# Two-layer graph attention: denominators summed into a row per target, own rows scaled on ScalarE, edge products ahead of weight copies

## The chip, the cores and the metric

The kernel runs on one core of a Trainium2 chip. The metric is the device time of one execution in microseconds; the median of several runs is compared.

## The reference

Two graph-attention layers run over 3327 nodes with 1024 features. Each layer adds its input to its output and normalizes every row.

```python
# layer 0, 8 heads of 128 features; adj has about 0.5% ones and ones on the diagonal
h = (x @ W0).reshape(C, 8, 128)
e = leaky_relu(alpha_src[:, :, None] + alpha_dst[:, None, :], 0.2)   # per head, C x C
attn = softmax(where(adj == 0, -inf, e), axis=-1)
x = layernorm(x + attn @ h)
# layer 1, one head
h = x @ W1
e = leaky_relu(h @ a1 + (h @ a2).T, 0.2)
x = layernorm(x + relu(softmax(where(adj > 0, e, -9e15), axis=1) @ h))
```

Since leaky_relu is a maximum of two linear terms, exp of it is a maximum of two products, so that the kernel needs an exponential only once per node and head, and multiplies and takes a maximum per edge.

## The kernel before

Nodes are cut into 26 tiles of 128 rows (`NT`). A tile of rows whose outputs are computed is called a target. The adjacency matrix is sparse, so the kernel first makes lists of edges, and then works edge by edge. There are three stages.

**Projection** (to about 552 us). For every tile, x is turned on TensorE and multiplied by W0 (L546), the result goes to `h0_d` in DRAM, and VectorE builds the edge lists `idx` and `tgt`. When half of the tiles are projected, a generator (`sums_so_far`) is run a step at a time between matmuls: for each of the first 13 targets (`EARLY`) it gathers the first two of the five edge blocks, sums the weighted rows into PSUM (L671), copies them to `z` (L726) and writes them to `half_d`; the softmax denominators of these blocks go to `dens`.

**Layer 0** (552 to about 1171 us). The order of the targets alternates between a late one (tiles 13 to 25, five blocks of edges) and an early one (tiles 0 to 12, three blocks left). A block is four gathers of 128 rows of `h0_d` (indirect DMAs issued by GpSimd, L1033); the last block, `EB`, is one gather. Five block buffers go round; a buffer is refilled when TensorE has finished with it. The instruction order of each engine is the order in which the code issues (`manual_schedule`), and every engine works its queue in order. For each target:

- `prepare` loads x rows and the target's own rows of `h0_d`, for an early one also the part sum `half_d`; `marks` (L1049, L1053) compares target numbers and gives the one-hot `oh`.
- `own` gives the weight `es` of each row for itself. For a late target ScalarE scales the own rows in eight steps (L1092); for an early one VectorE scales them and adds the part sum in eight steps (L1088). TensorE adds the result to the accumulators with an identity matmul, a half at the second and a half at the third block (L1126).
- `weights` makes a block's edge weights in the PSUM tile `way` (L1109, L1110), ScalarE copies them to `w` (L1112), and VectorE multiplies them with the one-hot to `e` (L1114).
- `sums` multiplies `e` with the gathered rows (L1145; L1134 for the last block) and sums the denominators (L1155, L1138): `w` is the stationary side, `oh` moves, so the result `den` has a row for each of 4 groups x 8 heads and a column for each target.
- `finish` masks the entries of `den` that do not belong together (L1167, `meets`), sums them by a matmul with `heads` (L1168) into a row per target, takes the reciprocal (L1171, L1172), scales the accumulators and adds x (L1177), normalizes, makes the two scores for layer 1 (L1184) and stores to `y_d`. It is a generator: `plans` says after which block of the next targets its next step is issued.

The same mask and heads matmul stand in `sums_so_far` (L707, L740, L737; L719 for the sums of denominators), put off to the next target by `owed`.

**Layer 1** (1171 to the end) gathers rows of `y_d` in the same way, sums them, and multiplies by W1 (L1289).

The two places that the change touches most, in the code before:

```python
den = ph.dd[:, P : 2 * P + H]                       # in sums_so_far
nc.tensor.matmul(den[: NG * H, :P], made[b][0].rearrange("p g h -> p (g h)"),
                 oh[:, b * NG : (b + 1) * NG, :].rearrange("p g t -> p (g t)"), ...)
```

Of the kernel before, what the change touches and what calls it, by code (L numbers as in the profile page):

```python
# [9 lines left out]
F32 = mybir.dt.float32  # L10
# [16 lines left out]
def kernel(  # L27
# [103 lines left out]
    io_t = const.tile([P, P], F32, name="io_t")  # L131
    meets = const.tile([NG * H, P], F32, name="meets")
    heads = const.tile([NG * H, H], F32, name="heads")

# [379 lines left out]
    with ExitStack() as own, tc.manual_schedule():  # L514
# [114 lines left out]
        def sums_so_far():  # L629
# [62 lines left out]
            yield  # L692
            owed = None
            for s in range(EARLY):
                acc = part.bank("L", [P, 2, 4, DH], "part")
                made = []
                for b in range(HB):
                    n = s * HB + b
                    val = src[n % 3]
                    made.append(weights(val, b, res[0], oh))  # L700
                    yield
                    if n:
                        fetch(n + 2)
                    yield
                    if b == 0 and owed:
                        met = part.sbuf("met", [NG * H, P], 1)
                        nc.vector.tensor_tensor(met, den[: NG * H, :P], meets, OP.mult)  # L707
                    yield
                    sums(acc, val, b, made[b][1], range(H // 2))
                    yield  # L710
                    sums(acc, val, b, made[b][1], range(H // 2, H))
                    if b == 0:
                        yield
                        if owed:
                            owed()
                        yield
                den = ph.dd[:, P : 2 * P + H]
# [21 lines left out]
            met = part.sbuf("met", [NG * H, P], 1)  # L739
            nc.vector.tensor_tensor(met, den[: NG * H, :P], meets, OP.mult)  # L740
            owed()

# [127 lines left out]
        for t in range(3, NT):  # L870
# [13 lines left out]
            if t == 11:  # L884
                ph.iota([P, P], [[1, P]], "io_t", base=1, dst=io_t)
                same = ident[: NG * H, : NG * H].rearrange("p (g h) -> p g h", g=NG)
                met = meets.rearrange("p (g t) -> p g t", g=NG)
                nc.vector.tensor_reduce(met[:, :, 0], same, AX.X, OP.max)
                nc.vector.tensor_copy(met[:, :, 1:], met[:, :, :1].to_broadcast([NG * H, NG, GT - 1]))
                nc.vector.tensor_reduce(heads, same.rearrange("p g h -> p h g"), AX.X, OP.max)  # L890
            if t == 16:
# [79 lines left out]
    def sparse(own):  # L971
# [84 lines left out]
        class Layer0:  # L1056
# [20 lines left out]
            def own(self):  # L1077

                t, h = self.t, self.h
                es = self.es = sbuf("es0", [P, H], 2)  # L1080
                nc.scalar.activation(es, sd0[:, t, 0, :], AF.Exp, scale=1 - SLOPE)
                nc.vector.tensor_tensor(es, es, h[:, D : D + H], OP.mult)
                nc.vector.tensor_tensor(es, es, h[:, D + H :], OP.max)
                nc.vector.tensor_scalar(es, es, loop[:, t : t + 1], None, op0=OP.mult)
                for n in range(H):
                    d = slice(n * DH, (n + 1) * DH)
                    if t < EARLY:
                        nc.vector.scalar_tensor_tensor(  # L1088
                            h[:, d], h[:, d], es[:, n : n + 1], self.half[:, d], op0=OP.mult, op1=OP.add
                        )  # L1090
# [11 lines left out]
            def weights(self, b):  # L1102
# [7 lines left out]
                nc.vector.tensor_tensor(wp, wp, s[:, :, D + H : D + 2 * H], OP.max)  # L1110
                w = sbuf("w", [P, NG, H], 4)
                nc.scalar.activation(w, wp if b < EB else wp.to_broadcast([P, NG, H]), AF.Copy)  # L1112
                e = sbuf("e", [P, H * P], 3).rearrange("p (g h t) -> p g h t", g=ng, h=H)
                nc.vector.tensor_tensor(  # L1114
                    e, oh.unsqueeze(2).to_broadcast([P, ng, H, wide]),
                    wp.unsqueeze(3).to_broadcast([P, ng, H, wide]), OP.mult,
                )
                self.made[b] = w, e

            def sums(self, b):  # L1120
# [4 lines left out]
                if j in (1, 2):  # L1125
                    nc.tensor.matmul(  # L1126
                        self.acc[j - 1].rearrange("p h d -> p (h d)"), ident, self.h[:, (j - 1) * HALF : j * HALF],
                        start=False, stop=False,
                    )
                elif j == 3:  # L1130
                    nc.tensor.matmul(self.acc[0][:, 0, :1], ident_b, none_b, start=False, stop=False)
                if b == EB:
                    for h in range(H):
                        nc.tensor.matmul(  # L1134
                            self.acc[h // 4][:, h % 4, :], e[:, 0, h, :], rowsof[:, 0, h, :],
                            start=False, stop=h % 4 == 3,
                        )
                    nc.tensor.matmul(  # L1138
                        self.den[: NG * H, :P], w.rearrange("p g h -> p (g h)"), self.oh2, start=False, stop=True
                    )  # L1140
                    return
# [10 lines left out]
                if j == 1:  # L1152
                    self.den = bank("S", [P, P + H], "den")
                for n in self.blocks[:2] if j == 1 else (b,):
                    nc.tensor.matmul(  # L1155
                        self.den[: NG * H, :P], self.made[n][0].rearrange("p g h -> p (g h)"),
                        self.oh[:, n * NG : (n + 1) * NG, :].rearrange("p g t -> p (g t)"),
                        start=n == self.blocks[0], stop=False,
                    )

# [3 lines left out]
            def finish(self):  # L1164

                met = sbuf("met", [NG * H, P], 2)
                nc.vector.tensor_tensor(met, self.den[: NG * H, :P], meets, OP.mult)  # L1167
                nc.tensor.matmul(self.den[:, P:], met, heads, start=True, stop=True)  # L1168
# [32 lines left out]
        class Target:  # L1201
# [21 lines left out]
            def own(self):  # L1223
# [5 lines left out]
                )  # L1229
                nc.vector.tensor_tensor(es[:, :1], es[:, 1:], loop[:, t : t + 1], OP.mult)  # L1230

            def fetch(self, b):
# [88 lines left out]
        def pipeline(items, fetches):  # L1321

            left, sent = [], [0]
            plans = {
                len(Target.blocks): ((), (2, 1), (1,), (1,), (1,), (1,)),
                len(Target.blocks) - HB: ((), (2, 1, 1), (1, 1), (1,)),
                Target: ((2,), (2, 1), (2, 1), (1, 1), (1, 1), (1,)),
# [30 lines left out]
            for i, it in enumerate(items):  # L1358
# [4 lines left out]
                for j, b in enumerate(it.blocks):  # L1363
                    if j == 0 and i:
                        items[i - 1].close()
                        if turn:
                            for _ in range(5):
# [189 lines left out]
```

## Time and profile before

| | us |
|---|---|
| median of 11 runs | 1801.81 (1797.72 to 1807.09) |
| the profiled execution's own time | 1803.52 |
| its span, first to last instruction | 1801.8 |

| stage (us) | length | PE busy | DVE busy | ACT busy | POOL busy | PE clock | GB/s |
|---|---|---|---|---|---|---|---|
| 280 to 552, projection with part sums | 272 | 259.4 | 220.4 | 126.4 | 184.6 | 0.99 | 281 |
| 570 to 690, layer 0 | 120 | 81.5 | 100.7 | 25.5 | 79.8 | 0.80 | 411 |
| 690 to 1090, layer 0 | 400 | 285.4 | 312.5 | 102.2 | 259.5 | 0.75 | 395 |
| 1090 to 1171, end of layer 0 | 81 | 41.7 | 40.9 | 14.7 | 49.7 | 0.77 | 338 |
| 1171 to 1801, layer 1 | 630 | 623.1 | 275.6 | 74.4 | 407.9 | 1.00 | 367 |

PE is TensorE's matmuls, PEld its weight loads, DVE VectorE, ACT ScalarE, POOL GpSimd, SP the engine that issues plain DMAs. "PE clock" is the share of full speed that the chip granted to TensorE. Lines such as L1114 are those of the kernel before. In the groups of instructions, `out<-in` names the tiles by the program's names. In the waits, "A <- B" says that A's engine sat idle until B had ended; the numbers are the total in us, how many times, and the longest. In the chain and the timeline, the first number is the start and the second the length. A float32 matmul appears as two passes, so "x2" is one matmul of the program.

### The profile page before, as it was taken

The page shows a single profiled execution, that of the slowest core. Times are in us where ns is not written, and L with a number is a line of the kernel's source. Part 1 is how long each engine was busy: PE and PEld are TensorE (multiplying, and loading weights), DVE is VectorE, ACT ScalarE, POOL GpSimd, SP SyncE. Part 2 cuts the span into 40 slices and gives each one's busy share as a digit, 9 for nine tenths or more (in the row PEclk, how much of TensorE's full clock was granted, in tenths as well). Part 3 has the DMA queues.
Part 4 walks back from the last instruction along what each step waited for, and adds up shares of the span by engine and source line. Part 5 has one row for each costly group of instructions (what it writes and reads, how often), then busy time and mean ns, then how long its engine had stood idle before and what let it go on. Part 6 is the DMA issues. An engine that isn't in the chain of part 4 may idle for free.

```text
span 1801.8 us, 35565 instructions
## 1 busy us (share of the span) xinstructions
PE 1548.4 (86%) x13168; PEld 909.3 (50%) x13168; DVE 1186.8 (66%) x3262; ACT 512.3 (28%) x1519; POOL 1109.8 (62%) x1580
## 2 busy tenths in 40 slices
PE   8899989999994677667777666499999999999998
PEld 4566656666663555455555454144444444444443
DVE  5799998898865888777777777344444444444443
ACT  5666654554431222222222222111111111111110
POOL 4533346677745766666666665677777667676650
PEclk9999999999996887867787768699999999999999
DMA  7456859999779999999999999999999999999980
GB/s 191 90 118 125 161 113 297 256 297 293 272 260 359 412 411 403 388 393 401 398 394 400 395 393 329 352 403 403 399 397 386 401 405 398 379 393 393 388 347 35
DMA packets 187319, 586.89 MB, mean 326 GB/s; under 512 B 36641, under 2 KB 46651, under 8 KB 187136
## 3 DMA queue, kind: packets, MB, share of 16 engines
q0 software_dynamic: 131056, 457.74, 71.3%
q1 hardware_dynamic: 55922, 126.52, 18.9%
q8 instruction: 107, 1.75, 0.4%
q14 instruction: 76, 0.62, 0.1%
q10 hardware_dynamic: 158, 0.26, 0.0%
HBM read 587.80 MB, written 51.23 MB: 355 GB/s over the span
## 4 chain that ended last, share of the span: by engine, by line
PE 55%; DMA 17%; DVE 15%; issue 5%; ACT 4%; POOL 3%; DVEq 0%; SPq 0%; ACTq 0%; POOLq 0%
PE mm L1289 21%; PE acc L1257 13%; PE mm L546 11%; DMA src<-h_d,idx 7%; DMA near<-h_d,idx 4%; PE acc L1145 3%; PE part L671 2%; PE tr L197 2%; ACT junk L350 2%; DVE e L1114 2%; PE acc L1126 1%; DMA own<-h_d 1%; DMA wt<-in_L_gnn_W_dram 1%; DVE top L309 1%; DMA src<-y_d,idx 1%
## 5 line engine op out<-in xcount | busy, mean ns | idle before, releaser
L546 PE MATMUL mm<-wt,xT 128*128 128x347 f32 (+1 forms) x1248 | 412.8, 472 | 3.4 <-DMA wt<-in_L_gnn_W_dram 3.4
L1289 PE MATMUL mm<-wt,xT 128*128 128x512 f32 x832 | 387.6, 604 | 0.0
L1033 POOL DMA_INDIRECT src<-y_d,idx x256 | 260.3, 1017 | 124.7 <-PE acc L1257 40.8
L546 PEld LDWEIGHTS mm<-wt,xT 128*128 128x128 f32 x1248 | 227.0, 193 | 120.6 <-issue 23.7
L1033 POOL DMA_INDIRECT src<-h_d,idx x184 | 196.7, 1069 | 110.2 <-PE acc L1145 23.2
L1289 PEld LDWEIGHTS mm<-wt,xT 128*128 128x128 f32 x832 | 149.7, 189 | 198.6 <-issue 193.6
L1292 DVE SCALAR_TENSOR_TENSOR o<-mm,y 128x512 f32<-128x512 f32 x52 | 36.0, 692 | 315.2 <-PE mm L1289 315.2
L1033 POOL DMA_INDIRECT near<-y_d,idx x160 | 163.7, 1023 | 61.5 <-issue 22.1
L1033 POOL DMA_INDIRECT near<-h_d,idx x120 | 131.1, 1093 | 70.0 <-PE acc L1145 21.1
L1114 DVE TENSOR_TENSOR e<-oh,way 128x1024 f32<-128x1024 f32 x104 | 127.1, 1222 | 58.7 <-ACT w L1112 58.3
L1145 PE MATMUL acc<-src,e 128*32 128x128 f32 x2944 | 124.4, 339 | 37.9 <-issue 19.2
L1257 PE MATMUL acc<-src,es 128*32 128x342 f32 (+1 forms) x1536 | 128.8, 470 | 25.4 <-DVE es L1248 25.4
L1145 PEld LDWEIGHTS acc<-src,e 128*32 128x32 f32 x2944 | 106.2, 138 | 72.4 <-issue 31.5
L200 ACT ACTIVATE xT<-tr 128x512 f32<-128x512 f32 x104 | 62.3, 600 | 249.3 <-PE tr L197 249.3
L1271 ACT ACTIVATE z<-y,ri 128x342 f32<-128x342 f32 (+1 forms) x78 | 39.5, 569 | 297.9 <-DVE ri L1267 297.9
L1145 PE MATMUL acc<-near,e 128*32 128x128 f32 x2048 | 88.8, 346 | 41.0 <-issue 18.1
L1112 ACT ACTIVATE w<-way 128x32 f32<-128x32 f32 x104 | 20.2, 194 | 330.0 <-DVE way L1110 324.9
L1145 PEld LDWEIGHTS acc<-near,e 128*32 128x32 f32 x2048 | 76.2, 141 | 66.2 <-issue 44.4
L641 POOL DMA_INDIRECT near<-h_d,idx x76 | 82.8, 1090 | 27.4 <-issue 18.3
L1257 PEld LDWEIGHTS acc<-src,es 128*32 128x32 f32 x1536 | 44.4, 112 | 98.4 <-issue 45.5
L1168 PE MATMUL den<-heads,met 32*128 32x8 f32 x52 | 14.2, 343 | 87.6 <-DVE met L1167 87.6
L350 ACT ACTIVATE junk<-ad 128x1664 uint8<-128x1664 uint8 x52 | 82.5, 1586 | 4.7 <-POOL ad L339 3.4
(247 smaller groups left out, 2587.9 us busy)
## 6 DMA issues: line engine op xcount, KB each, us to landing
h_d<-ht SPq DMA_DIRECT2D x26, 520.0 KB
own<-h_d SPq DMA_DIRECT2D x26, 520.0 KB
y_d<-y SPq DMA_DIRECT2D x26, 514.0 KB
y<-y_d SPq DMA_DIRECT2D x26, 514.0 KB
x<-in_x_dram SPq DMA_DIRECT2D x25, 512.0 KB
y<-in_x_dram SPq DMA_DIRECT2D x25, 512.0 KB
out_dram<-o SPq DMA_DIRECT2D x25, 512.0 KB
ad<-in_adj_dram POOLq DMA_DIRECT2D x25, 415.9 KB
```

Source lines behind the costliest of these rows:

```text
L197: nc.tensor.transpose(tr[:, k, :], src[:, (4 * g + k) * P : (4 * g + k + 1) * P], ident)
L200: nc.scalar.activation(part, tr, AF.Copy)
L350: nc.scalar.activation(junk, ad[:, n * THR : (n + 1) * THR], AF.Copy, accum_out=self.d[:, n : n + 1])
L546: nc.tensor.matmul(acc, xT[t][:, k, :], wt[:, k, CUTS0[c] : CUTS0[c + 1]], start=k == 0, stop=k == KT - 1)
L641: nc.gpsimd.indirect_dma_start(out=src[n % 3][:, g, :], out_offset=None, in_=h0_d[:THR, :], in_offset=bass.IndirectOffsetOnAxis(ap=idx[:, ...
L671: nc.tensor.matmul(acc[g * GT : (g + 1) * GT, h // 4, h % 4, :], e[:, g, h, :], vals[:, g, h, :], start=b == 0 and h % 4 == 0, stop=b == H ...
L1033: nc.gpsimd.indirect_dma_start(out=s[:, g, :w], out_offset=None, in_=table[:n, :], in_offset=bass.IndirectOffsetOnAxis(ap=idx[:, t, b * NG ...
L1114: nc.vector.tensor_tensor(e, oh.unsqueeze(2).to_broadcast([P, ng, H, wide]), wp.unsqueeze(3).to_broadcast([P, ng, H, wide]), OP.mult,)
L1145: nc.tensor.matmul(self.acc[h // 4][g * GT : (g + 1) * GT, h % 4, :], e[:, g, h, :], rowsof[:, g, h, :], start=first and h % 4 == 0, stop= ...
L1257: nc.tensor.matmul(self.acc[c][to, :m], es[:, g, :], s[:, g, CUTS[c] : CUTS[c + 1]], start=b == 0, stop=b == EB,)
L1271: nc.scalar.activation(z[:, cut], self.res[:, cut], AF.Copy, scale=ri[:, 1:2])
L1289: nc.tensor.matmul(acc, xT[:, k, :], wt1[:, k, half], start=k == 0, stop=k == KT - 1)
```

## The change

Four things are changed together.

- **Denominators.** One-hot marks are now the stationary side and the weights move, group by group: four matmuls of 8 columns for each block write a row per target. The constants `meets` and `heads`, the masks and the heads matmuls go, in layer 0 and in the projection's part sums; there `dens` is copied by ScalarE directly after `z`. `finish` has one step fewer, and `plans` and the count of steps at the turn to layer 1 are fitted to it.
- **Own rows.** They are scaled in eight steps by ScalarE for all targets, in a method `scale_own` that is issued after the weights of the second block. For an early target the part sum `half` is no longer added on VectorE: two more identity matmuls add it into the accumulators. The sum `es + dens` goes to a tile of its own, `total`.
- **Exponentials.** Those of `es` are made once for all targets at the start of layer 0 (`grows`).
- **Products.** `e` is issued before the copy `w`. Both read the PSUM tile `way`, and the program keeps the two engines apart there: the copy now waits for the product, and the next block's first write into `way` waits for the copy.

```diff
                 den = ph.dd[:, P : P + H]                      # sums_so_far
                 for b in range(HB):
-                    nc.tensor.matmul(
-                        den[: NG * H, :P], made[b][0].rearrange("p g h -> p (g h)"),
-                        oh[:, b * NG : (b + 1) * NG, :].rearrange("p g t -> p (g t)"),
-                        start=b == 0, stop=b == HB - 1,
-                    )
+                    for g in range(NG):
+                        nc.tensor.matmul(
+                            den[g * GT : (g + 1) * GT, :], oh[:, b * NG + g, :], made[b][0][:, g, :],
+                            start=b == 0, stop=b == HB - 1,
+                        )
...
                     nc.scalar.activation(z[:, n], acc[:, n], AF.Copy)
+                nc.scalar.activation(dens[:, s, :], den, AF.Copy)
...
-                def owed(s=s):
-                    nc.tensor.matmul(den[:, P:], met, heads, start=True, stop=True)
-                    nc.scalar.activation(dens[:, s, :], den[:, P:], AF.Copy)
...
+        grows = pool.tile([P, NT, H], F32, bufs=1, name="grows")
+        nc.scalar.activation(grows, sd0[:, :, 0, :], AF.Exp, scale=1 - SLOPE)
...
             def own(self):
-                es = self.es = sbuf("es0", [P, H], 2)
-                nc.scalar.activation(es, sd0[:, t, 0, :], AF.Exp, scale=1 - SLOPE)
-                nc.vector.tensor_tensor(es, es, h[:, D : D + H], OP.mult)
+                es, total = sbuf("es0", [P, 2, H], 2).rearrange("p a h -> a p h")
+                nc.vector.tensor_tensor(es, grows[:, t, :], h[:, D : D + H], OP.mult)
                 nc.vector.tensor_tensor(es, es, h[:, D + H :], OP.max)
                 nc.vector.tensor_scalar(es, es, loop[:, t : t + 1], None, op0=OP.mult)
+                self.es = self.total = es
+                if t < EARLY:
+                    self.total = total
+                    nc.vector.tensor_tensor(total, es, dens[:, t, :], OP.add)
+
+            def scale_own(self):
+                h = self.h
                 for n in range(H):
                     d = slice(n * DH, (n + 1) * DH)
-                    if t < EARLY:
-                        nc.vector.scalar_tensor_tensor(
-                            h[:, d], h[:, d], es[:, n : n + 1], self.half[:, d], op0=OP.mult, op1=OP.add
-                        )
-                    else:
-                        nc.scalar.activation(h[:, d], h[:, d], AF.Copy, scale=es[:, n : n + 1])
-                if t < EARLY:
-                    nc.vector.tensor_tensor(es, es, dens[:, t, :], OP.add)
+                    nc.scalar.activation(h[:, d], h[:, d], AF.Copy, scale=self.es[:, n : n + 1])
...
             def weights(self, b):
-                w = sbuf("w", [P, NG, H], 4)
-                nc.scalar.activation(w, wp if b < EB else wp.to_broadcast([P, NG, H]), AF.Copy)
                 e = ...                                        # the product, unchanged
+                w = sbuf("w", [P, NG, H], 4)
+                nc.scalar.activation(w[:, :ng, :], wp, AF.Copy)
...
             def sums(self, b):
                 if j in (1, 2):
-                    nc.tensor.matmul(acc[j - 1], ident, self.h[half j - 1], ...)
+                    for rows_ in (self.h, self.half) if self.t < EARLY else (self.h,):
+                        nc.tensor.matmul(acc[j - 1], ident, rows_[half j - 1], ...)
...
                 for n in self.blocks[:2] if j == 1 else (b,):
-                    nc.tensor.matmul(den[: NG * H, :P], w, oh of four groups, ...)
+                    for g in range(NG):
+                        nc.tensor.matmul(
+                            self.den[g * GT : (g + 1) * GT, :], self.oh[:, n * NG + g, :], self.made[n][0][:, g, :],
+                            start=n == self.blocks[0], stop=False,
+                        )
...
             def finish(self):
-                met = sbuf("met", [NG * H, P], 2)
-                nc.vector.tensor_tensor(met, self.den[: NG * H, :P], meets, OP.mult)
-                nc.tensor.matmul(self.den[:, P:], met, heads, start=True, stop=True)
-                yield
-                nc.vector.tensor_tensor(ri, self.den[:, P:], self.es, OP.add)
+                nc.vector.tensor_tensor(ri, self.den, self.total, OP.add)
...
-                len(Target.blocks): ((), (2, 1), (1,), (1,), (1,), (1,)),
-                len(Target.blocks) - HB: ((), (2, 1, 1), (1, 1), (1,)),
+                len(Target.blocks): ((), (2, 1), (1,), (1,), (1,), ()),
+                len(Target.blocks) - HB: ((), (2, 1), (1, 1), (1,)),
...
                     if j + 1 < nb:
                         it.weights(it.blocks[j + 1])
+                    if j == 0:
+                        it.scale_own()
                     it.sums(b)
```

The abbreviated lines in `sums` (`half j - 1`, `oh of four groups`) stand for the slices written out in the kernel.

More of the change, by code (lines that the diff above doesn't have):

```diff
@@ L131 @@
     io_t = const.tile([P, P], F32, name="io_t")
-    meets = const.tile([NG * H, P], F32, name="meets")
-    heads = const.tile([NG * H, H], F32, name="heads")
     near = [const.tile([P, NG, HG], F32, name=f"near{b}") for b in range(HB)]
@@ L692, in sums_so_far @@
             yield
-            owed = None
             for s in range(EARLY):
@@ L704, in sums_so_far @@
                     yield
-                    if b == 0 and owed:
-                        met = part.sbuf("met", [NG * H, P], 1)
-                        nc.vector.tensor_tensor(met, den[: NG * H, :P], meets, OP.mult)
                     yield
@@ L713, in sums_so_far @@
                         yield
-                        if owed:
-                            owed()
                         yield
-                den = ph.dd[:, P : 2 * P + H]
+                den = ph.dd[:, P : P + H]
                 for b in range(HB):
-                    nc.tensor.matmul(
-                        den[: NG * H, :P], made[b][0].rearrange("p g h -> p (g h)"),
-                        oh[:, b * NG : (b + 1) * NG, :].rearrange("p g t -> p (g t)"),
-                        start=b == 0, stop=b == HB - 1,
-                    )
+                    for g in range(NG):
[3 more added lines that the diff above has]
+                        )
                 z = part.sbuf("z", [P, 2, 4, DH], 1)
@@ L734, in sums_so_far @@
                 yield
-                def owed(s=s):
-                    nc.tensor.matmul(den[:, P:], met, heads, start=True, stop=True)
-                    nc.scalar.activation(dens[:, s, :], den[:, P:], AF.Copy)
-            met = part.sbuf("met", [NG * H, P], 1)
-            nc.vector.tensor_tensor(met, den[: NG * H, :P], meets, OP.mult)
-            owed()
         load_x(0)
@@ L885 @@
                 ph.iota([P, P], [[1, P]], "io_t", base=1, dst=io_t)
[L886 to L890, printed above, removed]
             if t == 16:
@@ L1125, in sums @@
                 if j in (1, 2):
[L1126 to L1129, printed above, removed]
+                    for rows_ in (self.h, self.half) if self.t < EARLY else (self.h,):
+                        nc.tensor.matmul(
+                            self.acc[j - 1].rearrange("p h d -> p (h d)"), ident, rows_[:, (j - 1) * HALF : j * HALF],
+                            start=False, stop=False,
+                        )
                 elif j == 3:
@@ L1137, in sums @@
                         )
-                    nc.tensor.matmul(
-                        self.den[: NG * H, :P], w.rearrange("p g h -> p (g h)"), self.oh2, start=False, stop=True
-                    )
+                    nc.tensor.matmul(self.den, self.oh2, w[:, 0, :], start=False, stop=True)
                     return
@@ L1152, in sums @@
                 if j == 1:
-                    self.den = bank("S", [P, P + H], "den")
+                    self.den = bank("S", [P, H], "den")
                 for n in self.blocks[:2] if j == 1 else (b,):
[L1155 to L1159, printed above, removed]
+                    for g in range(NG):
+                        nc.tensor.matmul(
+                            self.den[g * GT : (g + 1) * GT, :], self.oh[:, n * NG + g, :], self.made[n][0][:, g, :],
+                            start=n == self.blocks[0], stop=False,
+                        )
             def close(self):
@@ L1230, in own, with scale_own @@
                 nc.vector.tensor_tensor(es[:, :1], es[:, 1:], loop[:, t : t + 1], OP.mult)
+            def scale_own(self):
+                pass
             def fetch(self, b):
@@ L1366, in pipeline @@
                         if turn:
-                            for _ in range(5):
+                            for _ in range(4):
                                 next(left[i - 1])
```

## The prediction

> **What bounds the kernel now.** I read the busy shares by stage first, then the chain of waits inside the layer 0 stage, then the waits of that stage, then single instructions in the timeline. Columns of the stage table: stretch, length, busy time of PE, PEld, DVE, ACT, POOL (instructions), granted clock, DMA share, GB/s.
>
> ```profile
> 280.00:552.00 272.00, 259.42 (x2589) 174.63 (x2587) 220.41 (x600) 126.37 (x397) 184.61 (x361) 0.99 0.89 281
> ...
> 570.00:690.00 120.00, 81.53 (x1229) 59.64 (x1231) 100.73 (x246) 25.52 (x78) 79.79 (x73) 0.80 1.03 411
> 690.00:1090.00 400.00, 285.41 (x4172) 213.82 (x4168) 312.50 (x817) 102.23 (x302) 259.47 (x243) 0.75 1.01 395
> 1090.00:1171.00 81.00, 41.73 (x552) 23.42 (x548) 40.87 (x107) 14.69 (x38) 49.73 (x48) 0.77 0.91 338
> 1171.00:1801.00 630.00, 623.06 (x3526) 269.33 (x3518) 275.61 (x819) 74.40 (x152) 407.94 (x402) 1.00 0.94 367
> ```
>
> Projection (to 552) is PE's: 259 of 272 us busy. Layer 1 (from 1171) is PE's too, 623 of 630 us, and the diff does not touch what it runs; it moves as a block. Layer 0 lies between, and there DMA is nearly full: it holds 411 GB/s for 120 us, then only 395 for 400 us, then 338 in the hand-over to layer 1. If the 400 us ran at 411 they would take 400 x 395/411 = 384.4 us. So 15.6 us is all that faster engines can win in this part, and 81 - 81 x 338/411 = 14.4 us in the hand-over. The chain says what the missing share waits for:
>
> ```profile
> 681.41 2.20 DVE own L1088 x8
> 683.72 0.05 DVEq L1109
> 683.82 0.21 DVE way L1109
> 684.05 0.21 DVE way L1110
> 684.34 0.20 ACT w L1112
> 684.57 1.22 DVE e L1114
> 685.79 0.20 DVE met L1167
> 686.03 0.59 PE den L1168 x2
> 686.62 2.00 PE acc L1126 x2
> 688.63 2.66 PE acc L1145 x64
> ...
> 732.57 13.05 DMA src<-h_d,idx
> 745.67 0.70 issue
> 746.37 12.59 DMA src<-h_d,idx
> ```
>
> This is an early target. Own rows, weights, copy, product, mask and two kinds of matmul follow one another with no gap; from 732 the chain is gathers. It alternates between compute that frees a buffer and DMA that fills it, so shorter compute issues gathers sooner, but only up to the 411.
>
> ```profile
> PE den L1168 <- DVE met L1167: 58.6, 19, 4.7
> DVE e L1114 <- ACT w L1112: 41.2, 75, 2.3
> PE acc L1145 <- DVE e L1114: 23.3, 8, 4.2
> PEld acc L1145 <- DMA src<-h_d,idx: 9.0, 6, 1.5
> ```
>
> In 690 to 1090, DVE loses 41.2 us in 75 waits for the copy, and PE sits 58.6 us before the heads matmul. PE waits for products more than for gathers.
>
> **The change, part by part.** Prices of single instructions:
>
> ```profile
> 664.82 2.08 PE L1126 MATMUL acc<-own,ident 128*128 128x512 f32 x2
> 669.99 0.60 PE L1155 MATMUL den<-oh,w 128*32 128x128 f32 x4
> 670.52 1.12 PE L1126 MATMUL acc<-own,ident 128*128 128x512 f32 x2
> 671.58 1.95 PE L1145 MATMUL acc<-src,e 128*32 128x128 f32 x64
> 673.35 0.38 PE L1155 MATMUL den<-oh,w 128*32 128x128 f32 x2
> ```
>
> *Projection.* Removed on PE: 13 heads matmuls of two passes, 0.38 us each, 5.0 us busy, in a stage where PE is the path. Their masks (13 x 0.28 us on DVE) lie beside it: 0. Changed: per target the denominators go from 4 passes of 128 columns to 16 passes of 8 columns. From 0.60 and 0.38 us, one old pass costs 0.11 us, four 0.44. A new pass is not in the trace. Nearest row: 64 column-split passes in 1.95 us, 0.030 each, so 16 cost 0.49. The far bound is the old 0.11, 16 x 0.11 = 1.76, or +1.3 x 13 = +17 us. I take the 64-pass row, because it has the same column split and switching; that gives about +1. The `dens` copy now stands on ACT directly behind the two `z` copies (1.08 us), which take longer than the passes (0.49) that it waits for: 0. Sum -4 us, bounds -6 to +12.
>
> A rule speaks against the split. The Trainium skill, "TensorEngine Tiling (Array Packing)", Instruction Overhead: every matmul carries about 60 cycles of overhead, so that one output column costs as much as 60, and a factor should not be taken from a dimension that is already small. By it eight passes of 8 columns are 480 cycles where two of 128 were 256, 1.9 times as much; as an estimate 0.41 us for the old 0.22 per block, +0.19 x 26 blocks = +5 us here, and projection would be level instead of -4. No row of before has an 8-column pass of this shape.
>
> *DVE in layer 0.* An early target loses eight own-row steps (2.20), the mask (0.27) and three copy waits of 0.32: 3.4 us. A late one loses the mask, four waits of 0.32 and the one in which the copy stood behind eight ACT scalings (2.21 us): 3.8. Pair: 7.2 us of 41 (400 us hold 9.7 pairs). What comes instead: the first write into `way` of a block now waits for the previous block's copy, and all of DVE is queued behind it. Bounds: 0, or the same 0.32 each (41 us again). I take 0 for most, because between one product and the next write stands other work in most places: eight `y` steps (2.16 us), statistics (1.28) or a score product (1.22); the copy needs 0.2 us. The `es` exponentials (26 x 0.19 us on ACT) become one at the start, where ACT is idle until 561.7: 0. SP's and POOL's instruction orders are the same in both kernels; no DMA is added or moved past another.
>
> *ACT in layer 0.* 13 early targets add eight scalings, 2.44 us each, 32 us on an engine with 102 of 400 us busy. They hide, except that PE needs the first four.
>
> *PE in layer 0.* Out: 26 heads matmuls (0.59 us) with their wait. In: per early target two more identity matmuls, the first 2.08 us at the half clock, the second 1.12. Denominators: 8 x 0.030 = 0.24 for 2 x 0.11 = 0.22 per block: 0, bounds 0 to +0.66. The own rows now come behind the second block's product and copy. Before, from the product's end (685.79) to the sums (688.63) it took 2.8 us. After: copy 0.3, four scalings 1.2, own rows 2.08, half rows 2.08, 5.7 us for an early target, 3.6 for a late one. But the product itself ends 2.5 us sooner in both. With the second half's 1.12, an early target's PE path is 1.5 us longer, a late one's 1.7 shorter: level over a pair, while DVE's is 7.2 shorter. What is late next is DMA: at most 1.6 us a pair can be had. I take 1.0, since PE's path is not shortened: -10 us, bounds +4 (PE is the path in every early target, part of 13 x 1.5 shows) to -15.6.
>
> *Hand-over.* The own rows of the last targets land late (10.3 us of DMA in the chain), with nothing to gain there; behind them stand the scaling wait, two masks and heads matmuls (0.9 us each), and five copy waits (1.6). One `yield` fewer lets each target store its `y_d` a block sooner. I take -4, bounds +2 to -12.
>
> Sum: -4 - 10 - 4 = -18 us against the profiled execution's own 1803.5 (span 1801.8), 1785.5. That execution lies 1.7 above the median of the runs shown, so **1784** for the median.
>
> **Rivals.** *DMA hides it.* The rate stays at 395 because gathers themselves limit it in the mix after 690; for it: share 1.01 against 1.03 leaves little idle. Against: the same queues held 411 before. Body 0, projection -4, hand-over -1: 1797. The same time comes if DVE's new wait for the copy returns the 41 us.
>
> *Slower: own rows behind the product.* Where the second block's gather is what a target waits for, the old kernel had scaled own rows already; now scaling and four identity passes start only after the product, and the buffers of that block come free later. Then the product is not earlier, and the path is 2.9 + 1.1 = 4.0 us longer for an early target, 0.8 for a late one, 13 x 4.8 = 62 us if all were so. It decides if over a third of the targets are: +21, less 8 elsewhere, 1815. Against: PE's waits for gathers are 9.0 us in 6, against 23.3 for products.
>
> *It does less than it says* in the denominators: passes at 0.11 us each in both layers add 17 + 78 x 0.66 = 68 us of PE work; in projection 12 us net show. About 1800 if layer 0 still gains its 14.
>
> **How the numbers follow.** Forecast (1766 to 1794) 0.60; DMA hides it 0.16; dear denominators 0.08; slower 0.16. A change of 0.2%, 3.6 us, is about what a measurement of this kernel tells from none. Faster: 0.60, two thirds of the second, a third of the third: 0.74. Same: the rest of these two, 0.10. Slower 0.16. Low end: projection -6, body -15.6, hand-over -12, 1768. High end takes in the two middle cases and the near edge of the slow one, 1805.
>
> **What would show it.** Right: L1167 and L1168 gone; the 8-column passes near 0.03 us; waits of products for copies gone, few of `way` for `w`; ACT busier by 27 us; GB/s from 690 on nearer 411; layer 1's length unchanged. Wrong: layer 0's rate still 395 with DVE idle; PE waiting for ACT scalings in early targets; projection longer than 552.

## The result, and the profile after

The changed kernel took 1792.17 us (median of 8 runs, 1789.0 to 1795.26), the kernel before 1802.91 us in the same comparison: a ratio of 0.9943, 95% interval 0.9931 to 0.9954. It is faster by 10.7 us, where 18 were forecast. The profiled execution's span is 1790.2 us against 1801.8. In the tables below a stage ends where the next one's first instruction starts, read from the trace:

| us from the span's start | before | after |
|---|---|---|
| first matmul of the part sums | 280.6 | 277.1 |
| end of the last part sum | 549.3 | 538.3 |
| first gather of layer 0 | 558.8 | 547.7 |
| first sum of layer 1 | 1133.0 | 1119.0 |
| first `mm` of layer 1 | 1171.9 | 1159.8 |
| end | 1801.8 | 1790.2 |

At the first gather of layer 0 the changed kernel is already 11.1 us ahead. Of these, 3.5 us stand before the first part sum; in the profiles of this case that point lies anywhere between 276.5 and 281.2 us, also in kernels with the same projection (280.6 in the kernel before, 276.6 in the kernel before with four buffers), so they are not put down to the change. The part sums themselves take 261.3 us for 268.7, 7.4 less. From the first gather to layer 1's first `mm` it takes 612.1 us where the kernel before took 613.1, and layer 1 is 630.4 for 629.9. So nearly all of the lead stands before layer 0; 14 of the 18 us had been forecast for layer 0 and its end.

The stage table of the changed kernel answers to the first fence of the prediction, shifted by the 3 to 12 us that it is ahead (stretch, length, busy time of PE, PEld, DVE, ACT, POOL, granted clock, DMA share, GB/s):

```profile
277.00:541.00 264.00, 249.33 (x2717) 169.01 (x2716) 217.10 (x586) 124.98 (x396) 184.54 (x361) 0.99 0.91 288
558.00:678.00 120.00, 80.76 (x1297) 59.12 (x1297) 93.16 (x218) 33.16 (x100) 78.22 (x74) 0.76 1.03 407
678.00:1078.00 400.00, 269.55 (x4609) 197.46 (x4608) 288.95 (x720) 123.66 (x364) 255.87 (x244) 0.80 1.01 395
1078.00:1160.00 82.00, 38.91 (x512) 21.52 (x511) 35.60 (x100) 14.19 (x37) 50.98 (x50) 0.73 0.94 355
1160.00:1790.00 630.00, 622.40 (x3510) 269.09 (x3510) 275.47 (x819) 74.40 (x152) 406.86 (x401) 1.00 0.94 365
```

In the 400 us of layer 0, DVE has 23.6 us less work than before (288.95 for 312.50) and PE is busy 15.9 us less, but the last two columns stand where they stood: share 1.01, 395 GB/s. The transfers did not get faster. PE's 15.9 us are not all work removed: the identity matmuls for the part sums add 31.6 us, while the 10.7 us of heads matmuls and 11.4 of the 26.8 us of denominators are gone, and a pass of the sums of `src` rows took 314 ns on the mean for 348, at a granted clock of 0.80 for 0.75. The waits of this stretch:

```profile
PE acc L1110 <- ACT own L1077: 71.5, 18, 6.0
...
DVE way L1092 <- DMA src<-h_d,idx: 43.3, 16, 4.9
PE acc L1127 <- DVE e L1095: 40.1, 14, 5.3
...
DVE way L1092 <- DMA near<-h_d,idx: 20.8, 6, 4.6
...
DVE es L1064 <- DMA own<-h_d: 14.3, 11, 3.0
...
DVE way L1092 <- DMA end<-h_d,idx: 9.3, 3, 3.2
```

and those of DVE in the kernel before, 690 to 1090 us, that are not shown above:

```profile
DVE es L1082 <- ACT es L1081: 8.9, 16, 0.6
...
DVE way L1109 <- DMA end<-h_d,idx: 6.6, 3, 2.4
DVE way L1109 <- DMA src<-h_d,idx: 5.0, 6, 1.5
...
DVE way L1109 <- DMA near<-h_d,idx: 0.9, 1, 0.9
DVE es L1082 <- DMA own<-h_d: 0.7, 1, 0.7
```

Both waits that the change was aimed at are gone: PE's 58.6 us before the heads matmul, DVE's 41.2 us for the copy. In their place PE waits 71.5 us for ScalarE's own rows (L1077 is the scaling, L1110 the identity matmul in the changed kernel), and DVE waits for gathers. Its waits for `src`, `near`, `end` and `own` rows add to 43.3 + 20.8 + 9.3 + 14.3 = 87.7 us in this stretch; before, the same waits added to 6.6 + 5.0 + 0.9 + 0.7 = 13.2. DVE was freed of 23.6 us of work and of 41.2 + 8.9 us of waits for ScalarE (the copy and the exponentials), 73.7 us together, and waited 74.5 us more for DMA.

The chain of waits shows one target (start, length, what):

```profile
700.27 13.61 DMA src<-h_d,idx
714.06 0.21 DVE way L1092
714.29 0.21 DVE way L1093
714.60 1.22 DVE e L1095
715.91 0.20 ACT w L1100
716.19 0.11 issue
716.30 0.98 ACT own L1077 x3
717.32 3.54 PE acc L1110 x4
720.86 1.87 PE acc L1127 x63
```

A gather of 13.6 us comes first; the weights start 0.2 us and the product 0.7 us after it has landed, and copy, scaling, identity matmuls and sums follow. The long row of DVE steps that stood at the head of the same chain before (own rows, mask) is no longer in it.

### The profile page after: what moved, and what is told of

Same layout as the page of the kernel before. It is cut to its first block, busy times and chain, and to the rows that moved or that the text cites. A ratio compares the mean times of both kernels' runs of the same rounds, so it can differ in the third digit from the quotient of the medians.

```text
span 1790.2 us, 36777 instructions
## 1 busy us (share of the span) xinstructions
PE 1515.5 (85%) x13766; PEld 883.3 (49%) x13766; DVE 1148.3 (64%) x3116; ACT 539.3 (30%) x1598; POOL 1106.0 (62%) x1580
## 4 chain that ended last, share of the span: by engine, by line
PE 44%; DMA 17%; DVE 4%; ACT 1%; issue 1%; POOL 0%; DVEq 0%; SPq 0%; POOLq 0%; ACTq 0%
PE mm L1270 21%; PE acc L1238 13%; DMA src<-h_d,idx 7%; PE acc L1110 4%; DMA near<-h_d,idx 4%; PE acc L1127 4%; DMA own<-h_d 4%; DVE e L1095 2%; ACT own L1077 1%; PE tr L195 1%; DMA src<-y_d,idx 1%; PE acc L1118 1%; DVE pr L982 1%; DMA near<-y_d,idx 1%; DMA av<-in_L_gnn_a_dram 1%
## 5 line engine op out<-in xcount | busy, mean ns | idle before, releaser
L1110 PE MATMUL acc<-own,ident 128*128 128x512 f32 x104 | 82.4, 884 | 108.5 <-ACT own L1077 104.3
L1016 POOL DMA_INDIRECT near<-h_d,idx x120 | 127.0, 1058 | 72.3 <-PE acc L1127 21.4
L1127 PE MATMUL acc<-src,e 128*32 128x128 f32 x2944 | 111.5, 314 | 29.1 <-DVE e L1095 28.7
L1100 ACT ACTIVATE w<-way 128x32 f32<-128x32 f32 (+1 forms) x104 | 20.0, 193 | 385.0 <-DVE e L1095 171.9
L1127 PEld LDWEIGHTS acc<-src,e 128*32 128x32 f32 x2944 | 94.4, 128 | 60.7 <-DVE e L1095 39.5
L1127 PE MATMUL acc<-near,e 128*32 128x128 f32 x2048 | 80.1, 322 | 34.6 <-DVE e L1095 22.6
L639 POOL DMA_INDIRECT near<-h_d,idx x76 | 82.5, 1086 | 26.8 <-issue 17.7
L1127 PEld LDWEIGHTS acc<-near,e 128*32 128x32 f32 x2048 | 68.1, 131 | 58.7 <-DVE e L1095 29.3
```

What stands on the lines that cost most here:

```text
L639: nc.gpsimd.indirect_dma_start(out=src[n % 3][:, g, :], out_offset=None, in_=h0_d[:THR, :], in_offset=bass.IndirectOffsetOnAxis(ap=idx[:, ...
L1016: nc.gpsimd.indirect_dma_start(out=s[:, g, :w], out_offset=None, in_=table[:n, :], in_offset=bass.IndirectOffsetOnAxis(ap=idx[:, t, b * NG ...
L1110: nc.tensor.matmul(self.acc[j - 1].rearrange("p h d -> p (h d)"), ident, rows_[:, (j - 1) * HALF : j * HALF], start=False, stop=False,)
L1127: nc.tensor.matmul(self.acc[h // 4][g * GT : (g + 1) * GT, h % 4, :], e[:, g, h, :], rowsof[:, g, h, :], start=first and h % 4 == 0, stop= ...
```

## The experiments

All were compared with the kernel before on the same chip. Three of them ran on a slower chip, where the kernel before took 1897.67 us; these three are read only against that.

**The projection alone** (the kernel before with the new `sums_so_far`, nothing else):

```diff
-                    nc.tensor.matmul(den[: NG * H, :P], w of four groups, oh of four groups, ...)
+                    for g in range(NG):
+                        nc.tensor.matmul(den[g * GT : (g + 1) * GT, :], oh[:, b * NG + g, :], made[b][0][:, g, :], ...)
...
-                    nc.tensor.matmul(den[:, P:], met, heads, start=True, stop=True)
```

> The kernel before with one part of the change alone: the part sums of the projection sum their denominators straight into a row per target (no masks, no heads matmuls there); layer 0 keeps the old way. Theory A (nearly the whole gain of the changed kernel is the projection's: 13 heads matmuls of 0.38 us and 13 x 0.3 us for the cheaper sums of denominators, about 9 us; layer 0 is held by its transfers): 8 to 11 us faster than before, ratio 0.994 to 0.9955, layer 0 as long as before (614 us from its first load of re to the first matmul of layer 1). Theory B (the projection gained 4 to 5 us as forecast, the rest of the 11 us that the two profiles differ by is scatter between executions, and layer 0 gained the remaining 5): 4 to 5 us faster, ratio about 0.9975.

Measured: 1794.83 us for 1802.18, ratio 0.9957 (0.9943 to 0.9971), 7.7 us less by the ratio. The part sums run from 281.2 to 541.5 us, 260.3 us for 268.7 before; layer 0 takes 613.4 us, as before. The changed kernel stood at 0.9943 in the first comparison and at 0.9956 in a second one (below), 10.7 and 7.6 us between the medians: most of the gain, perhaps all of it, comes from this edit.

**Layer 0 alone** (the changed kernel with the old `sums_so_far`):

```diff
-                    for g in range(NG):
-                        nc.tensor.matmul(den[g * GT : (g + 1) * GT, :], oh[:, b * NG + g, :], made[b][0][:, g, :], ...)
+                    nc.tensor.matmul(den[: NG * H, :P], w of four groups, oh of four groups, ...)
...
+                    nc.tensor.matmul(den[:, P:], met, heads, start=True, stop=True)
```

> The changed kernel with the projection's part of the change undone (masks and heads matmuls as before there); all of the change in layer 0 stays. Theory A: no different from before, 1801 to 1804 us, ratio 0.999 to 1.001. Theory B: 5 to 6 us faster than before, ratio 0.997.

Measured: 1800.38 us, ratio 0.9991 (0.9978 to 1.0004): about 1.6 us less, and no difference is inside the interval. Its layer 0 takes 611.4 us. The two parts add to 7.7 + 1.6 = 9.3 us, which lies between the 7.6 and the 10.7 of the whole.

**Own rows scaled first.** Is it the new wait of PE for ScalarE that holds layer 0 back? Here the scaling is issued ahead of the second block's weights:

```diff
+                    if j == 0:
+                        it.scale_own()
                     if j + 1 < nb:
                         it.weights(it.blocks[j + 1])
                     ...
-                    if j == 0:
-                        it.scale_own()
```

> The changed kernel with one order turned back: ScalarE scales the own rows before the second block's weights, so that TensorE need not wait for the second block's product and copy to add the own rows. Theory A1 (layer 0 is held by its transfers at 395 GB/s; a wait more or less on TensorE moves nothing): as the changed kernel, ratio to before 0.993 to 0.9955, GB/s from 690 us on still 395, though TensorE's 71.5 us of waits for the scaling go. Theory C (VectorE's gain was given back by TensorE's new wait for the scaling): 5 to 12 us faster than the changed kernel, ratio 0.988 to 0.991, GB/s towards 405.

Measured: 1791.76 us, ratio 0.9951 (0.9938 to 0.9964), layer 0 611.4 us: as the changed kernel. Its waits in 678 to 1078 us:

```profile
PE acc L1127 <- DVE e L1095: 117.2, 42, 5.5
DVE way L1092 <- DMA src<-h_d,idx: 41.9, 15, 5.3
...
DVE way L1092 <- DMA near<-h_d,idx: 32.8, 12, 4.8
```

PE's wait for the scaling has gone, and PE waits for products instead, 117.2 us, while DVE waits for gathers as long as ever. So the two waits of PE are read as one idle time under two names. The rate in 690 to 1090 us is 393 GB/s, as in the changed kernel in that stretch. The new wait costs nothing here that the intervals tell.

**Half of every gather.** If transfers hide the gain, the gain must show when the transfers are lighter. In these three kernels a gather of layer 0 brings 512 of a row's 1040 columns; the edge weights are taken from the first 16 of these, and the sums over the other columns read what stands there, zeros that GpSimd sets at the start in three of the five block buffers and old rows in the other two. The computation is thereby another one; each engine's instructions are the same in kind and size.

```diff
-                    out=s[:, g, :w], out_offset=None, in_=table[:n, :],
+                    out=s[:, g, :c], out_offset=None, in_=table[:n, :],      # c = 512 in layer 0
```

On the kernel before:

> The kernel before with half the gathered bytes in layer 0: each gather there reads the first 512 of 1040 columns of a row, and edge weights are taken from the row's first 16 columns; the second half of the rows and the true weights are left out, every instruction of the engines stays. Both theories: layer 0 is then held by the engines and not by DMA. It should fall from 614 us to 26 targets x 17 to 21 us, 450 to 560 us, and its length is the engines' own pace for the old order.

On the changed kernel:

> The same halving of gathers in the changed kernel (second half of the rows and true weights left out). Theory A1 (the change does make the engines faster, and full transfers hide it): layer 0 is 40 to 90 us shorter than in the halved kernel before (3 to 7 us a pair of targets, from VectorE's 7.2 us a pair). Theory C (TensorE's new wait for the scaling takes the place of VectorE's): within 15 us of the halved kernel before.

On the kernel that scales own rows first:

> The changed kernel with halved gathers and with the own rows scaled before the second block's weights. Theory A1: with the engines in charge the order shows; up to 20 us either way of the halved changed kernel. Theory C: at least 40 us shorter than the halved changed kernel.

| | us | ratio to the kernel before | layer 0 |
|---|---|---|---|
| kernel before, half gathers | 1777.34 | 0.9858 (0.9833 to 0.9883) | 578.3 |
| changed, half gathers | 1706.59 | 0.9456 (0.9432 to 0.9481) | 523.8 |
| own rows first, half gathers | 1706.85 | 0.946 (0.9437 to 0.9484) | 521.1 |

The stage rows of the kernel before with half gathers:

```profile
690.00:1090.00 400.00, 286.84 (x4355) 214.83 (x4357) 324.14 (x848) 107.10 (x319) 270.56 (x251) 0.79 0.78 250
```

and of the changed kernel with half gathers:

```profile
680.00:1040.00 360.00, 254.67 (x4646) 192.62 (x4638) 296.00 (x745) 126.96 (x373) 276.85 (x259) 0.87 0.87 291
```

With DMA at a share of 0.78 the old kernel's layer 0 still takes 578.3 us from its first gather. Because the zeros are set first, this gather stands 17 us behind the last part sum instead of 9.5, so 7 us of the difference to 613.1 are only a later start of the count. From the first sum of layer 0 to layer 1's first `mm` it is 580.9 us for 608.6, and the whole run is 27.4 us shorter: the engines by themselves set a pace only some 28 us short of that with full gathers. The change makes this pace 54.5 us faster (54.2 from the first sum: 526.6 for 580.9). With full gathers 1.0 us of the 54.5 is seen (0.5 from the first sum: 608.1 for 608.6). So the change does make the engines faster, and the transfers hide it. The granted clock differs too, 0.87 for 0.79 in the rows above, so part of the 54.5 may be faster passes and not less work; this was not separated.

The changed kernel with half gathers meets a third limit, the issuing of gathers on GpSimd. Its waits for PE to free a buffer, in the old kernel and in the changed one (same stretches as above; total, times, longest):

```profile
POOL src L1036 <- PE acc L1148: 41.2, 41, 4.3
POOL near L1036 <- PE acc L1148: 28.3, 27, 4.5
```

```profile
POOL src L1019 <- PE acc L1130: 10.7, 35, 0.3
...
POOL near L1019 <- PE acc L1130: 8.5, 28, 0.3
```

In the changed kernel no such wait is longer than the 0.3 us that lie between any two gathers. 258 gathers of 1.07 us, with 0.3 us before each, fill 353 of the 360 us. With full gathers the same sum is about 330 of 400 us. So 54.5 us is rather a lower bound of what the change is worth to the pace, and the order of the scaling, which again makes no difference (521.1 for 523.8), could not have shown much there.

**Three runs on the slower chip.** The own rows were added behind the block's sums instead of ahead of them (at the second and third block; at the last one, where the accumulators close, still ahead):

```diff
-                if j in (1, 2):
+                if j == 2 and b == EB:
                     add_own()
...                                              # the block's sums
+                if j in (1, 2):
+                    add_own()
```

> The changed kernel with the identity matmuls of own and half rows issued behind the second and third block's sums instead of ahead of them (ahead only where that block is the last). TensorE then frees the block's buffer without waiting for ScalarE's scaling. Theory D (what is left in layer 0 is the transfers' own rate; no order of the engines moves it): as the changed kernel, ratio to before 0.993 to 0.9955, layer 0 612 us. Theory E (the dips below 411 GB/s are gathers that wait for a buffer, so a buffer freed 1 to 4 us sooner shows): layer 0 5 to 15 us shorter, ratio 0.986 to 0.991.

the products and sums of heads 4 to 7 were left out in all blocks but a target's first and last (half of the outputs' terms are then missing):

```diff
+                m = H if b in (self.blocks[0], EB) else H // 2
...
-                for h in range(H):
+                for h in range(H if first else H // 2):
```

> The changed kernel with half the engines' edge work in the blocks between a target's first and last: products and sums of heads 4 to 7 are left out there; all transfers stay full. Theory D: layer 0 stays at 608 to 613 us. Theory E: with VectorE 0.6 us and TensorE 1 us or more shorter per block, buffers come free sooner and layer 0 falls by 10 to 25 us.

and four block buffers went round instead of five:

```diff
-        NS = 5
+        NS = 4
```

> The changed kernel with four block buffers instead of five. Theory D: eight gathers in flight fill the transfers, and four buffers hold sixteen; up to 10 us longer. Theory E: every target's turnaround shows: 30 us longer or more, with GB/s in layer 0 well under 395.

| | us | ratio to the kernel before | layer 0 | GB/s, 700 to 1100 us |
|---|---|---|---|---|
| own rows behind the sums | 1887.56 | 0.9942 (0.992 to 0.9964) | 648.2 | 377 |
| heads 4 to 7 left out | 1876.08 | 0.9877 (0.9847 to 0.9908) | 638.5 | 388 |
| four buffers | 1865.20 | 0.9824 (0.9797 to 0.9852) | 642.3 | 388 |

On this chip PE itself is late. The largest of PE's waits in 700 to 1100 us, in the kernel with own rows behind the sums:

```profile
PE acc L1130 <- issue: 86.0, 204, 1.1
```

"issue" is time in which PE waited for nothing that the profile shows, here 0.4 us at a time between the passes of a sum. In 690 to 1090 us the changed kernel has no such wait in its profile on a faster chip. So these three do not test what holds layer 0 there. The kernel without heads 4 to 7 has a layer 0 that is 9.7 us shorter than with own rows behind the sums (the two also add the own rows at different places), which may be fewer passes to issue as much as less work. Own rows behind the sums came out at the changed kernel's ratio, with the changed kernel itself not run there. Four buffers were expected to cost and were the fastest of the three. There the first gather of layer 0 starts 10 us earlier than with own rows behind the sums (565.2 us for 575.2), but the first sum 9 us later (587.7 for 578.8), so the start is not what made it faster; from that sum to layer 1's first `mm` it takes 619.9 us for 644.6. Why is open.

**Four buffers on a faster chip.** The last three runs stood side by side where the kernel before took 1801.93 us: the changed kernel, and either kernel with four buffers (the edit above).

> The changed kernel unaltered, so that the two kernels with four block buffers of this call have it beside them on the same chip. Both theories expect about 0.994 of the kernel before (0.992 to 0.996), with the first gather of layer 0 landing behind the store of the part sums (its issue 8 to 9 us after the last part sum).

> The changed kernel with four block buffers instead of five in layer 0. Theory F (with four buffers the first gathers of layer 0 no longer wait for the store of the last part sums to land): the first gather starts about 10 us earlier than in the changed kernel of this call, the layer 0 stage itself is of equal length within 3 us, ratio to the kernel before 0.985 to 0.990. Theory G (fewer gathers outstanding make the transfers themselves faster, whatever the start): the layer 0 stage is at least 6 us shorter between its first gather and layer 1's first matmul, ratio below 0.985. If five buffers are needed to cover the gathers (the old expectation): slower than the changed kernel, 0.997 or more.

> The kernel before with four block buffers instead of five in layer 0, nothing else changed. Theory F: the gain belongs to the start of layer 0 and not to the change, so the kernel before gains it as well: first gather about 10 us earlier, ratio 0.993 to 0.996. Theory G: 0.990 or less, with a higher rate in 690 to 1090. If the slower engines of the kernel before need the fifth buffer: 1.002 or more.

| | us | ratio to the kernel before | last part sum ends | first gather | layer 0 | first sum of layer 0 | from it to layer 1's first `mm` |
|---|---|---|---|---|---|---|---|
| changed, five | 1794.29 | 0.9956 (0.9943 to 0.9969) | 537.5 | 546.0 | 612.6 | 551.0 | 607.6 |
| changed, four | 1790.44 | 0.9936 (0.9923 to 0.995) | 538.5 | 541.5 | 618.9 | 554.7 | 605.7 |
| before, four | 1809.54 | 1.0044 (1.0031 to 1.0057) | 546.6 | 549.0 | 625.3 | 564.5 | 609.8 |

With five buffers a wait stands at the turn to layer 0, in the changed kernel in 530 to 570 us:

```profile
DVE y L965 <- DMA half_d<-z: 11.3, 1, 11.3
```

With four it is not there, and the first gather starts 3.0 us after the last part sum instead of 8.5; in the kernel before it is 2.4 instead of 9.5. That half of the expectation held. The other did not: counted from the first gather, layer 0 gets 6.3 us longer with four buffers in the changed kernel, and 12.2 in the kernel before (against the 613.1 of its first profile). Most of this is the start itself. The gathers begin earlier, but the first sum comes later, 16.2 us after the last part sum instead of 13.5 (in the kernel before 17.9 for 14.1), because DVE now waits for the tile `re`, the target's factors of the edge weights:

```profile
DVE way L1092 <- DMA re<-re_d: 11.4, 1, 11.4
```

Its load, issued at 546.5 us, with gathers already on their way, is there 6.4 us later; in the changed kernel's first profile it took 2.5 us. From the first sum on, the changed kernel takes 607.6 us with five buffers and 605.7 with four, the kernel before 608.6 and 609.8: the fifth buffer shows no price there. So the changed kernel gains nothing that the intervals tell apart (0.9923 to 0.995 against 0.9943 to 0.9969), and the kernel before loses, 3.9 us of it in the start. No version was found that is surely faster than the changed kernel.

## Why the prediction was right, and where its steps were not

The sign and the range of the forecast held, in part by luck. The largest term, 14 of the 18 us, came to about 1, and the projection gave nearly twice its term; the sum came within 8 us because the two errors stood against each other. Two of the three signs that the prediction named for being wrong were seen: layer 0's rate still 395 with DVE waiting, and PE waiting for the scalings.

**Projection, forecast -4: mis-sized, -7.7 by itself.** The groups of PE instructions, kernel before (line, engine, operation, tiles, shape, count, busy time and mean ns, idle before):

```profile
L719 PE MATMUL dd<-oh,w 128*32 128x128 f32 x52 | 7.8, 273 | 0.0
L737 PE MATMUL dd<-heads,met 32*128 32x8 f32 x26 | 5.0, 262 | 1.5 <-ACT place_of L371 0.8 <-DVE met L740 0.4 <-ACT cnt L392 0.3
```

and the changed kernel:

```profile
L712 PE MATMUL dd<-w,oh 128*32 128x8 f32 x208 | 3.8, 176 | 1.0 <-issue 1.0
```

The 5.0 us of heads matmuls went, as forecast. The failed term is the price of the denominators: 0.030 us a pass was taken from the 64 passes in 1.95 us, making +1. In the timeline (start, length), first the changed kernel, then the kernel before:

```profile
317.74 0.29 PE L712 MATMUL dd<-w,oh 128*32 128x8 f32 x16
317.96 0.56 PE L544 MATMUL mm<-wt,xT 128*128 128x346 f32 x1
```

```profile
296.08 0.60 PE L719 MATMUL dd<-oh,w 128*32 128x128 f32 x4
296.61 0.56 PE L546 MATMUL mm<-wt,xT 128*128 128x346 f32 x1
...
310.91 0.38 PE L737 MATMUL dd<-heads,met 32*128 32x8 f32 x2 [0.26 <-ACT cnt L392]
311.22 0.88 PE L546 MATMUL mm<-wt,xT 128*128 128x347 f32 x1
...
547.35 1.95 PE L671 MATMUL part<-far,e 128*32 128x128 f32 x64
549.12 0.60 PE L719 MATMUL dd<-oh,w 128*32 128x128 f32 x4
```

From its own start to the next matmul's start a run of 16 passes takes 0.22 us, 0.014 each. In the kernel before, by the same reading, four passes of 128 columns take 0.53 us (296.08 to 296.61) and the two heads passes 0.31 (310.91 to 311.22). Per target that is 0.53 + 0.31 - 0.22 = 0.62 us, x 13 = 8.1 us, and 7.7 were measured. The 64-pass row had 128 columns in each pass where the new ones have 8, and these cost half as much. A price from start to start would also have shown that the old passes cost more than the 0.44 that was taken. The last two rows show why one price for a shape misleads: 64 passes of the same shape as the old ones take 1.77 us from start to start, 0.028 each, where the old four take 0.13 each. In the code the 64 go round the four column positions of `acc` and the old four all stand in one; that this is the cause was not tested by itself.

The Trainium skill, "TensorEngine Tiling (Array Packing)", Instruction Overhead, had spoken against the split: about 60 cycles for every matmul however few its columns, as an estimate +5 us. The estimate did not come true: 16 passes of 8 columns, 0.22 us from start to start, come out below 4 passes of 128 columns, 0.53. It had added the passes one after another and had priced the old ones at 0.11. Whether a matmul here carries the 60 cycles is not settled: the 16 passes are 8 matmuls of the program on four column positions, and the runs show only the 0.22 us of them all. The ends of matmuls in a trace are modelled, but the starts and the 7.7 us of the whole do not rest on them.

**Layer 0, forecast -10 for the body: failed, about -3, of which the hand-over took 2 back.** From the first gather to layer 1's first sum it was 574.2 us before and is 571.3 after. The engine side was read rightly. DVE's own-row steps and masks, 2.20 + 0.27 + 0.27 us a pair, were to go: 9.7 x 2.74 = 26.6 us, and 23.6 went. The waits for the copy went and did not come back as waits of `way` for `w`. The 54.5 us with half gathers are 4.2 us for each of 13 pairs, half of the 7.2 worked out for DVE; since GpSimd sets the pace there, they do not say how much of the 7.2 is real. The step that failed is the one after it: "What is late next is DMA: at most 1.6 us a pair can be had. I take 1.0". The 1.6 came from 411 GB/s, a rate that was read in the first 120 us and taken as attainable in the 400 us behind them. Neither the lighter engines nor the other order of scaling nor four buffers moved that rate: in 690 to 1090 us it was 395 before, and 393, 393 and 394 in the changed kernel, with own rows first and with four buffers. The share of 1.01 in the same row said that little idle time was left in the transfers; it was named for the rival and given too little weight. Why the later stretch holds 395 and the first one 407 to 411 was not found out.

The Trainium skill, "DMA: Bandwidth & Descriptors", Specifications, gives 435 GB/s as the ceiling of the fabric to SBUF and about 358 GB/s as the HBM limit of a core. The rows of layer 0 up to the hand-over lie between the two, at 393 to 411, so neither figure gives the 395; by the first, layer 0 would have had even more to win.

Two small readings of the prediction were off and moved nothing. Its far bound for DVE's new wait, "the same 0.32 each (41 us again)", is 75 x 0.32 = 24 us; the rest of the 41.2 were the waits behind eight scalings. And the 9.0 us for gathers that it set against PE's 23.3 are PEld's.

**Hand-over, forecast -4: failed.** From layer 1's first sum to its first `mm` it was 39.0 us before and is 40.8 after. The rate in the last 82 us rose from 338 to 355 GB/s, which the stage as a whole does not show. It was not tested by itself.

**The rivals.** *DMA hides it* is what layer 0 did; its 1797 is 5 us too slow only because it shared the projection's -4. With -8 there and the same -1 for the rest it gives 1793. *Slower: own rows behind the product* has its mechanism in the trace, 71.5 us of PE waiting for the scaling, but the scaling put first moved no time that the intervals tell, so no price of it was seen. *Dear denominators* fell with the 0.22 us.

## What to carry to other kernels

A stage whose DMA share is 1.0 is priced by its bytes at the rate of its own stretch, not at the best rate of another stretch; an engine's saving there turns into waiting for gathers, and halving the gathers shows in one pair of runs that it is hidden and how large it is at least, until the next limit, here the issuing of gathers. Two lengths are compared from the first work of a stage, not from its first gather, when an edit moves that gather. Where an engine is the path, as PE in the projection, a few tenths of a microsecond per target are worth their full sum. Price short matmuls by their own shape and from start to start, and read a wait that replaces another as a possible new name for the same idle time until it is taken away.

## What the runs showed of the hardware that was not expected

- Sixteen float32 passes of 8 columns in four column positions took 0.22 us from start to start, less than half of four passes of 128 columns (0.53 us), at a granted clock of 0.99.
- Two chips ran the same program (the kernel before) 5% apart: 1897.67 us against 1801.93. On the slow one PE lost 86.0 us in 204 stalls named "issue" in 400 us of layer 0 of the kernel with own rows behind the sums, at 377 GB/s.
- Halving the bytes of every gather took 28 us off layer 0 of the kernel before, counted from its first sum, and 82 off the changed one (608.1 to 526.6), while the change alone took 0.5: two limits lay close together, and lowering either one alone shows little.
- A gather of 128 rows kept GpSimd for about 1.07 us and 0.3 us lay before the next one, with half rows too; 258 of them in 360 us left it nearly no time to spare.
